# Joining each stage's linear term with its cube on DVE, and moving sums to POOL and ACT, in a two-phase recurrence and attention kernel

## The chip, the cores and the metric

The kernel runs on one core of a Trainium2 chip, in one launch. The metric is the device time in microseconds (us), as the median of several executions. A core has five engines that work side by side and wait for each other by semaphores: TensorE (PE; its weight loads are shown apart as PEld), VectorE (DVE), ScalarE (ACT), GpSimd (POOL) and SyncE (SP), which issues the DMAs. SBUF is the on-chip memory, PSUM the smaller memory that PE accumulates in.

## The reference

Two layers follow each other, each with a "condition" part and a feed-forward part, and both add to a residual. The first condition part is a time recurrence: 32 steps of a fourth-order Runge-Kutta scheme over a state q (128 x 256) with a companion p.

```python
def _derivative(q, p, drive, coupling, bias):
    i_couple = jnp.tanh(q) @ coupling.T
    dq = q - q ** 3 / 3.0 - p + drive + i_couple + bias
    dp = EPSILON * (q + ALPHA - BETA * p)
    return (dq, dp)

def _rk4_step(q, p, drive, coupling, bias):
    dq1, dp1 = _derivative(q, p, drive, coupling, bias)
    dq2, dp2 = _derivative(q + 0.5 * DT * dq1, p + 0.5 * DT * dp1, drive, coupling, bias)
    dq3, dp3 = _derivative(q + 0.5 * DT * dq2, p + 0.5 * DT * dp2, drive, coupling, bias)
    dq4, dp4 = _derivative(q + DT * dq3, p + DT * dp3, drive, coupling, bias)
    q_next = q + DT / 6.0 * (dq1 + 2 * dq2 + 2 * dq3 + dq4)
    p_next = p + DT / 6.0 * (dp1 + 2 * dp2 + 2 * dp3 + dp4)
    q_next = jnp.clip(q_next, -CLAMP, CLAMP)
    p_next = jnp.clip(p_next, -CLAMP, CLAMP)
    return (q_next, p_next)
...
x = x + _L0_ffn_ref(_L0_cond_ref(cond_2048, cond_2048, x, L0_cond_coupling, L0_cond_bias), L0_ffn_w_gate, L0_ffn_w_up, L0_ffn_w_down)
x = x + _L1_ffn_ref(_L1_cond_ref(x, cond_2048[:, None, :], L1_cond_W_emb, L1_cond_b_emb, L1_cond_g_norm, L1_cond_W_qkv, L1_cond_g_q, L1_cond_g_k, L1_cond_W_out), L1_ffn_w_gate, L1_ffn_w_up, L1_ffn_w_down)
```

The q of every step goes through a feed-forward network whose activations and weights are quantized in blocks of 32 (`_L0_ffn_ref`: gate, up, silu, down). The second layer is an attention over the 32 time steps with 16 heads of 16, in which queries and keys are normed and multiplied with weights `g_q` and `g_k`, and a feed-forward network with a Hadamard transform and 8-bit activations (`_L1_cond_ref`, `_L1_ffn_ref`).

## The kernel before

**Two phases.** Phase one runs the 32 time steps (`step`, L853) and, for each, the first feed-forward network (`ffn0`, L1238), the norm of the second layer and its value projection. Phase two (`tokens`, L1472) runs 32 groups of 128 tokens through attention and the second feed-forward network.

**A planner sets the order.** The functions do not issue instructions; they call `add(engine, cost, fn, reads, writes, ...)`, which records an item with its engine, an expected cost in us and the tiles that it reads and writes. `Work.run` then builds one order for all engines: a list scheduler that takes, at each point, the item with the least wanted time among those that can start. The wanted times are kept in the source as two long strings, `TIMES`, one for each phase. Costs serve this order alone; they change nothing in an instruction. An item marked `port=True` is kept from running beside another marked item; all tile operations of POOL carry the mark, and of DVE those that read two SBUF tensors or a large one in place. Where the planned PE is idle over 0.45 us, `keep_warm` puts matmuls on zeros in front of the next item (L1707).

**A stage of a step.** Each of the four stages has a PSUM tile `ps[i]` (256 columns) that collects the stage's sums: a first sum written by DVE (`nest`, L828, a `scalar_tensor_tensor`: in0 * scalar + in1), the drive and bias through PE (`inputs`, L860), the coupling (8 matmul records at L897, on tanh from ACT at L890), and the stage's own linear term, the state itself times a constant, through an eye matmul (`plus`, L881, the matmul at L883). Square (ACT, L891) times the state (POOL, L904) is the cube. A `nest` then joins `ps[i]` and the cube to the next state (`q2`, `q3`, `m4`), and the step ends with two saturating adds (L948) that give the new p (`z`) and the new q (a `states` tile). `p` and the sums `x`, `w`, `z` lie in slots of `ps_sum`, in PSUM, so that every `nest` has a PSUM tensor among its inputs.

```python
nest(ps[0], q, 2 * K[0] / h, p, rank)
inputs(0, RAW)
nest(ps[1], p, h / 2 * P2[0] / K[1], q, rank)
inputs(1, HALF_STEP)
nest(x, p, P3[0] * h / K[2], q, rank)
cube = slope(0, q)
nest(w, p, -LAST[0] / LAST[1], q, rank)
nest(z, p, -END[0] / END[1], q, rank)
nest(q2, ps[0], R2 * h / 2, cube, rank)
plus(1, 0, q2)
cube = slope(1, q2)
```

**Around it.** In `ffn0` POOL multiplies with block scales (L1258, L1301, L1309) and with the norm's gain (L1350), DVE takes maxima, products and clips (L1007, L992, L999, L1252, L1232, L1285). During the first steps the weights of the first network are quantized too, with POOL operations on 1024 columns (L1045, L1057, L1066). In `tokens` the queries are multiplied with `g_prod`, the product of the two weights, on POOL (L1512) before DVE transposes them (L1520); the exponential (L1552) and the silu (L1624) on ACT lie in different function tables, and each change between them is an ACT_TABLE_LOAD.

Of the kernel before, what the change touches and what calls it, by code (L numbers as in the profile page):

```python
# [15 lines left out]
AF = mybir.ActivationFunctionType  # L16
# [5 lines left out]
P = 128  # L22
# [83 lines left out]
class Work:  # L106
# [27 lines left out]
            "BIBKCNC9BWBVCiCWBuCTCaBzBfD7DjGGByDyEJEgEgE_CpGBEKEXFqF_GYEsFHGLGMFjGCGbGoIXHjHKIBHpHUJJKOL6J_LVJFJX"
            "K_KcJXKgKuMYNRMV9WBgBdDSCbDpCEDUCmCjCECLDqDtDpCID3D9CXBoDoCsEJE0EIDODjDYDOCpEAE5DVDdEUEuDLDqE5DdD-FQ"
            "FPH3DPFkFMFRFqFhE0FmFeGFGxHqI8GdGmHPHhIRIGH0H6I6IVJ6IuJUK4M6LILrM8ORL-MDN4LxLaMyObNWRFOFA3C-DQFJDdFU"
            "DxFOEIEhDiFeFjFbFPEFEoF0EIEzFKEoFOFAFmEfFHFkE0DVF-FlEwF1GJG8EnGBGkEuFSGOGLFvGGHzIJH9HkHGHhG_IHJPIYIv"
            "J5INJbIYJ5KNK3JbK6K1MDLZJsKJOhPONUNGR7MtQJO8QuNkRANpRrOOSDODDFEMF2GPFpGBFnGiFuGkFUGQGeGgGCFvHAHfG4H8"
            "HOF_GVHmHYG9GcGxGDHJH7H2G5GTIPH2GTHDH5GFGVGYHrJcHzIjItIbIcIOK5KfK8JeJVKPKRJzKMJCLKM5MALOKoM9L5NeMYN5"
            "NbSLO4O9ReN0RzPMRkPvRKOES7O-QUQ6GUG_H-H1H0HZGpHLH0GaGpGlHKH4HLGpHvGwHhH-HXI2HoHcHPHiH7H_IBIEHhHsHNIN"  # L140
            "I8IJHzHNHTI5HhIRIcNsJZJzJDIJKEKULHLIJoKkLFLULpMAMMN2MIMSMPMoMvNZNgOINkONMVRYPxQ4RaRASmRgS4RBSiQYS7SW"
            "RePRHjI7HvIgIgIHHuHxIJJ2JNJqIuIkJFJdIzIuIoJzItJ2IjJ2JWJqHRIUJxIOIbInJ7KKJvJpJTIkIyJSJQKgLJNXLxMLMELd"
            "NJMGMiOTMUMyPXNmNbN2O1QpNaO2PaPDPyQ8Q1PpPdQhN_RvRtRzRnQ1RGRdRwRGQsSBS2TJSgSdIQJ8JPJbKvKbKLKiKIKKJ_J_"
            "JlKTKPJwKWKdKTJMKyJqJhKWKQL0L2K4KVKiKnKaKPLJMNL2LZLWLALILsLGLcLwMfMrNPNXNVNxO1N-O6OMRnQIPdOKOURhQvQL"
            "QpQWR4R4RBRoS3RoPnRESTSJSnRiSVTfSyTESWThTKUyU7S8L8KQK8LrLMMKM5LxNBLbL9MsL_MrMNLsPCNvLjLwLeLuMfM1MYMz"
            "N_OCLsMzOHOdLtMfMLNHMBPhQLMZNCMzMuQUODNcOkNzPQOYQUOeOWOoS6QGS6OYPeSGRIROSVR-RnRkRiR-T3RWRXSrTZUDTeRm"
            "TuUWU0VsTfUGUvV_WRVOLIO1MMM4NAMONpMuQOQXN8NLMvMrNANGRfR5MnNEMuNUNLNJNoNmQiR8MxO-RPR4MaO5OVOeMxRNRcNq"
            "PuOFP9S8OVP-QeQbPzROP-QTPlR8S3S0RAQHRfT0SJSUSnShRrT0SaRqTtTpRsUZVGVxWhUNW0WuW2XUWrWXWfW7WoWlLZRHRDP9"
            "NOOhNcOiRERrNTPkPmQ8PvO8PxQiNlPwOyOCPVPuPjNuRVRCOZQvRlRWO3NeQJQiOrQlRROmQiPvQTPkPBR9QGRHR7RsR5QrSRSC"
            "RlT4SnSZShRbTVUNTmTUTfVWULVGUXUQSIXFX3XAY7XFXvYRZHYSYPXgZ8X-ZaYOMcQxRiQaPvQjPgQqRjRLPGQVQvQTQvQ3R7RZ"  # L150
            "QuQyQNQKR4QYSPQvRRRxQDRORhRPRBRdRTRTRMR5RmRNRAS2RWRERLRsRyRySNRmRURuSiTGTFUxUuTHU0UMUwVVVWVnVgVzVyWD"
            "WvWgTaZWXdXnZ2XYYzWlZIZXZoYDbEYCc9Z-O7S9RPRkRRRCRnS7Q_RMQwQPRvRqSNRmRQRARKRVReS9R_RQSTSAQ-RGRiRNRURN"
            "SISBTMSmRqSQSESQSZTDTaSOT9V2UsU1USUsTrQhUGUNUMW4W8UUUvV8X6X6XhXlXVY7XfX9YdYOYFb3YMYkcyYSbtZjcCahcmYw"
            "cQZVdGYkQHRnRFTpRoU4T2TnSdSaSZU6URUDTaTXTEShTXToTgShTuUAU3TJSfSyTjUWTFTETLTtV8UvTOTWTYTWUdUvVCSfU0VX"
            "V-VgVtWmWCSFW0WhWPY0YOWOXGWlYyYxZpYZZbZYaPa8Yma6badgZhZudJaEcvafd0bacsafd6c3dsdGQrSzSaUqU4ViU1VZU9T_"
            "TwVnVmVOV6UCULULUbUQV8UIVoW7VyUVUUUZUiV0V8V0UTU-W6WuVJVGVyVjWaWQW_WhVdX4Y0XSXGYOX0VoXAXQX_YBZ4XOXjaC"
            "XhY4YjZgbCZVZZZvZhaPcCdtbEbLeTcjeRcRegcpdwc9f5djfke8RmUUUzWVVoWFWWWrWGWIWIWXWtXMXPWOWiWuWGWkXOWPXgXX"
            "XdVyWiX6VqXMXLXEWyWpXyXyWVX4XHWkYiXgY1YGXLXVXnYRXpXYa_YdY5YPZaY_YfY8YdaQZbaabRb9ambobeZOdJapayfec8cj"
            "f1dvf4d_f_eGf5e7fue2fygARyWZWwXZXKXTX9YAXMYFWuVjXbWoYHXHYdYAXCZSXFX7Y0XJXQX8YuZIXMZEa7ZeXiXEXpXXXhZ6"
            "ZGXkZbYIYRX6Y8YWYwZBYoZ3XpYKYdYubbbabiYbZTc3bPbncxdQand4bsc5cvbvdKg0d8dtf3dqeqhFf4f7fGeafLeCfuiJY3YC"  # L160
            "YsX_XmYVYCY5ZMZGY9ZPYMYTYcXeb0b0Y8YTYJXuYPYvYvY4bebnYCZkbOaVY5YPYqa8YBbbbvY9ZKZia4Y-YyaqataobEbNaGZ9"
            "a4amd8cJcKb2bUctdFdneEeYe_e-f9eTdUf7eugffKetg2gogyghfzhFh1gFgSgWgqk1Y6ZWaPZ-YgZxYRaJbyc3Y3XRaYakbEYt"
            "c3cXYVXRb3Zja9bLb3Z2cyd0YaYzdcdWZSZKbdbeZ3djdMZEYsblcDc7aJczcwbwcKc3c_cObwctetd6dqczdHgKe8f3fYfpfAf9"
            "fwfgg9ggg3gAh1g9gzk8gshfhBiWgzhzhGisibl7YucBcCbUaKceaCbpcVcbaEa3cbbScGajd3dLZmbFbOaqbvcAb_akdBdWaUdM"
            "csdcbKb1bvcVbOdkdDb6d2ckbte3bxcsd7dBeTdmdee9dbd_fXgggOeceqfDfkebfYf0hDgMgrgKgtgwjjhBhwidi9jRhnjEiXiX"
            "iHiwiIjij6jHZkdAdOc1bKcdbxcJeBfdbrcBcYcad2buewe6c6dMcAc7cQcZddd3e1ead8d1egeeczdceGfod7eVf5dldGfLfJfH"
            "drezf7fAemgJgIg2gOgfgQgOg_gMgOgogjgShzhHhzgXj1ichVibl2j3jGjcjDm2jAjujgiNjYkak4kGktmqareEfAdwdleadOei"
            "fafkdqe9ere4dQdZewetdSejetdWdWeOefdoeJe-eTf6eUfJeGe8eZf2e1fTgpf9fleKfeggflgQgBfFgUg4gOi1h7hlhPh8hBh_"
            "hXh8hviNimhfjAiGkCjZikjHlikJk6khl0mOkwiQlIkkkZkolim4luo5dNfDf8fCeMf7f1fLfsfDf7fgfgfgfdfXeufFfIfzf-fS"
# [12 lines left out]
        (
# [361 lines left out]
def kernel(  # L544
# [283 lines left out]
    def nest(dst, in0, scalar, in1, rank, op1=ADD):  # L828
# [4 lines left out]
    b_p = Buf(ps_sum)  # L833
    add(
        DVE, 0.335,
        lambda: nc.vector.tensor_scalar(b_p.ap, condT, -ALPHA / BETA, -1.0, ADD, MULT),
        [b_condT], [b_p], rank=FIRST,
    )

# [930 lines left out]
```

## Time and profile before

| | |
|---|---|
| runs of the kernel | 794.51 us median of 3 (794.3 to 797.28) |
| the profiled execution | 793.31 us, its span 791.5 us |
| granted TensorE clock | 0.997 |
| PE busy | 742.4 us, 94% of the span |
| DVE busy | 693.8 us, 88% |
| POOL busy | 593.7 us, 75% |
| ACT busy | 533.9 us, 67% |
| eye matmuls L883 | 256 records, 78.7 us busy |
| cubes on POOL L904 | 128 (96 on `slim`, 31 on `states`, one on `condT`); the 96 take 771 ns each |
| ACT_TABLE_LOAD | 16 at L1552 and 16 at L1624, 1283 ns each |

The span is the time from the first to the last instruction of one execution; the rest of the execution's time lies around it. Busy time of an engine counts an instant once, however many records cover it; records of one engine overlap in its pipeline, so start-to-start distances are the better price where instructions stand close. An f32 matmul appears as two records. A group row gives the source line, the engine, the operation, what it writes and reads, the count, busy us and mean ns of one, and the idle time before it with what ended it.

### The profile page before, as it was taken

Reading aid. Unit: us, or ns where it says so; the run is one execution under the profiler, and the core shown is the slowest. Engines: PE = TensorE matmul, PEld = TensorE weight load, DVE = VectorE, ACT = ScalarE, POOL = GpSimd, SP = SyncE. Lnnn points to the kernel's source line nnn. Section 1 sums busy time; section 2 is a strip of 40 time slices with the busy share of each in tenths; the row PEclk is TensorE's granted clock in tenths of the full one; section 3 lists DMA queues with packets and bytes.
Section 4 is the critical chain, followed back from the end, with each engine's and each line's share of the span. In section 5 each row is a group of like instructions: output and inputs, shape, how many; then the busy total and the mean of one; then the engine's idle time right before and its main releaser. Section 6 shows DMA issues by size and latency. Waiting matters only on the chain.

```text
span 791.5 us, 26294 instructions
## 1 busy us (share of the span) xinstructions
PE 742.4 (94%) x10493; PEld 575.0 (73%) x10493; DVE 693.8 (88%) x1730; ACT 533.9 (67%) x1087; POOL 593.7 (75%) x963
## 2 busy tenths in 40 slices
PE   6879999999999999999887999999999999999996
PEld 5656688888888887788655566676777677777775
DVE  7888999999998998899837989899988999898894
ACT  4334467776766778998542577777877857688864
POOL 7968999878987788688727778877788788786700
PEclk9999999999999999999999999999999999999999
DMA  8222344323333253465330111433232532322552
GB/s 254 101 41 41 68 88 101 84 69 82 82 86 80 69 153 103 126 133 115 75 104 17 25 34 27 77 64 70 58 73 60 97 61 80 66 63 63 86 114 67
DMA packets 138522, 64.44 MB, mean 81 GB/s; under 512 B 103456, under 2 KB 137376, under 8 KB 138400
## 3 DMA queue, kind: packets, MB, share of 16 engines
q1 hardware_dynamic: 138400, 62.77, 34.6%
q8 instruction: 82, 1.34, 0.7%
q14 instruction: 40, 0.33, 0.1%
HBM read 25.77 MB, written 12.85 MB: 49 GB/s over the span
## 4 chain that ended last, share of the span: by engine, by line
PE 23%; DVE 16%; ACT 5%; POOL 3%; issue 3%; DMA 1%; ACTq 0%; DVEq 0%; POOLq 0%
PE ps_one L1483 4%; DVE wide L1647 4%; PE ps_two L1658 4%; PE ps_two L1616 3%; DVE tiny L1432 3%; PE ps_one L1560 3%; PE ps_one L1530 2%; PE ps_two L794 2%; DVE wide L1631 2%; PE ps_one L1583 2%; POOL wide L1647 1%; PE ps_one L1681 1%; ACT wide L1666 1%; DVE tiny L1545 1%; DVE tiny L1496 1%
## 5 line engine op out<-in xcount | busy, mean ns | idle before, releaser
L1647 POOL TENSOR_TENSOR wide<-wide 128x512 f32<-128x512 f32 x116 | 148.8, 1303 | 34.3 <-DVE wide L1647 16.8
L897 PE MATMUL ps_stage<-slim,coup 128*128 128x128 f32 x1024 | 139.1, 279 | 2.6 <-ACT slim L890 2.0
L897 PEld LDWEIGHTS ps_stage<-slim,coup 128*128 128x128 f32 x1024 | 127.8, 191 | 16.6 <-ACT slim L890 11.8
L904 POOL TENSOR_TENSOR slim<-slim,slim 128x256 f32<-128x256 f32 x96 | 74.0, 771 | 28.6 <-ACT slim L891 25.5
L883 PE MATMUL ps_stage<-slim,eye 128*128 128x256 f32 x256 | 78.7, 394 | 4.4 <-DVE slim L831 4.2
L1309 POOL TENSOR_TENSOR wide_bf<-mid,tiny 128x512 bf16<-128x512 fp8e4 x62 | 65.7, 1064 | 4.0 <-DVE mid L1232 3.7
L1301 POOL TENSOR_TENSOR mid<-mid,tiny 128x512 f32<-128x512 f32 x62 | 64.6, 1050 | 3.3 <-DVE tiny L999 1.7
L1658 PE MATMUL ps_two<-had_ffn,wide 128*128 128x128 f32 x512 | 63.7, 278 | 1.6 <-ACT wide L1653 0.8
L1658 PEld LDWEIGHTS ps_two<-had_ffn,wide 128*128 128x128 f32 x512 | 60.1, 192 | 5.8 <-ACT wide L1653 2.5
L1483 PE MATMUL ps_one<-w_qkv_sb,xnT 128*128 128x512 f32 x128 | 62.4, 616 | 0.7 <-ACT v_pad L1380 0.7
L890 ACT ACTIVATE slim<-slim 128x256 f32<-128x256 f32 x96 | 39.4, 410 | 29.0 <-DVE slim L831 28.7
L891 ACT ACTIVATE slim<-slim 128x256 f32<-128x256 f32 x96 | 39.1, 407 | 25.4 <-DVE slim L831 25.3
L883 PEld LDWEIGHTS ps_stage<-slim,eye 128*128 128x128 f32 x256 | 40.9, 190 | 20.9 <-DVE slim L831 17.2
L1647 DVE TENSOR_TENSOR wide<-wide 128x512 f32<-128x512 f32 x76 | 55.2, 762 | 0.0
L1666 ACT ACTIVATE wide<-ps_two,magic,tiny 128x1024 f32<-128x1024 f32 x32 | 38.6, 1205 | 24.2 <-DVE tiny L1440 14.6
L1232 DVE SCALAR_TENSOR_TENSOR mid<-mid,ps_sum 128x512 fp8e4<-128x512 f32 x64 | 43.3, 678 | 4.0 <-POOL mid L1301 3.8
L1432 DVE TENSOR_REDUCE tiny<-ps_two 128x1 f32<-128x1024 f32 x32 | 38.9, 1216 | 8.6 <-PE ps_two L1658 7.8
L1285 DVE TENSOR_TENSOR mid<-ps_gu,mid 128x512 f32<-128x512 f32 x64 | 43.5, 683 | 2.2 <-ACT mid L1281 1.8
L1653 ACT COPY wide<-ps_two 128x1024 f32<-128x1024 f32 x32 | 32.3, 1010 | 18.3 <-PE ps_two L794 17.7
L831 DVE SCALAR_TENSOR_TENSOR slim<-ps_stage,slim 128x256 f32<-128x256 f32 x96 | 40.1, 417 | 4.8 <-PE ps_stage L897 3.2
L1616 PEld LDWEIGHTS <-slim_bf 128*128 128x128 bf16 x256 | 23.9, 98 | 27.6 <-issue 7.4
L1281 ACT ACTIVATE mid<-ps_gu 128x512 f32<-128x512 f32 x64 | 37.7, 592 | 8.6 <-PE ps_gu L1273 8.3
(285 smaller groups left out, 2153.2 us busy)
## 6 DMA issues: line engine op xcount, KB each, us to landing
v_dram<-v_pad SPq DMA_DIRECT2D x32, 136.0 KB, 1.9
v_pad<-v_dram SPq DMA_DIRECT2D x32, 136.0 KB, 2.5
x_step<-in_x_dram SPq DMA_DIRECT2D x32, 128.0 KB, 2.1
x_add<-in_x_dram SPq DMA_DIRECT2D x32, 128.0 KB, 2.5
x_dram<-slim SPq DMA_DIRECT2D x32, 128.0 KB, 1.8
out_dram<-slim SPq DMA_DIRECT2D x21, 128.0 KB, 1.7
raws<-in_L_ffn_w_gate_dram SPq DMA_DIRECT2D x4, 512.0 KB, 5.7
raws<-in_L_ffn_w_up_dram SPq DMA_DIRECT2D x4, 512.0 KB, 6.5
```

Source lines behind the costliest of these rows:

```text
L883: PE, cost, lambda: nc.tensor.matmul(ps[i].ap, lhsT=eyes[eye], rhs=src.ap, start=False, stop=True, skip_group_check=True),
L897: nc.tensor.matmul(ps[i].ap[:, sl], lhsT=coup[COUP[i]][:, c, sl], rhs=two(th.ap)[:, c, :], start=False, stop=True, skip_group_check=True,)
L904: POOL, 0.685, lambda: nc.gpsimd.tensor_tensor(sq.ap, sq.ap, qi.ap, MULT),
L1285: DVE, 0.6, lambda act=act, it=it, pu=pgu[1]: tt(it.ap, pu.ap, act.ap, MULT),
L1301: lambda it=it, ks=ks, eng=eng: eng.tensor_tensor(blocks(it.ap), blocks(it.ap), spread(binv.ap[:, ks], BLOCK), MULT),
L1309: lambda b8=b8, ks=ks, sl=sl, eng=eng: eng.tensor_tensor(blocks(bq.ap[:, sl]), blocks(b8.ap), spread(bscl.ap[:, ks], BLOCK), MULT),
L1432: lambda: nc.vector.tensor_reduce(am.ap[:, 0:1], src.ap[:, :n], AX.X, ALU.max, apply_absolute_value=True),
L1483: nc.tensor.matmul(pqk.ap, lhsT=xnT_flat[:, c, tok], rhs=w_qkv_sb[:, c, : 2 * N], start=(c == 0), stop=(c == NC - 1),)
L1616: nc.tensor.matmul(pgu.ap[:, n * HALF : (n + 1) * HALF], lhsT=two(aT.ap)[:, c, :], rhs=w[:, sr, c, :], start=(c == 0), stop=(c == NC - 1),)
L1647: eng.tensor_tensor(dv[:, :, e, :], sv[:, :, 0, :], sv[:, :, 1, :], op)
L1658: nc.tensor.matmul(pfh.ap[:, sl], lhsT=iT.ap[:, sl], rhs=had_ffn, start=True, stop=True)
L1666: lambda: nc.scalar.activation(br.ap, pfh.ap, AF.Identity, bias=magic, scale=bs.ap[:, 0:1]),
```

## The change

In each stage the linear term no longer goes through PE: it is joined with the cube, so that the DVE operation computes (square + own) * state with a constant `own` for each stage. That takes the cube from POOL to DVE, and three of the four eye matmuls away; `plus(3, 2, q3)` remains. The first sum of a step becomes a scaled copy of p on ACT. The sum `x` is made by a scaling on ACT and an add on POOL, the first `z` (now `z1`) by a subtraction on POOL. For that p is carried times a constant `LAM`, and `p`, `x`, `z1` and the new p lie in SBUF (`slim`). In phase two the product with `g_prod` is no longer made by POOL on the queries but by ACT on the transposed queries, with a column of weights per partition (`g_col`, made once by three small DVE operations). Some recorded costs differ (0.27 to 0.307 for the drives, for instance), and both strings of wanted times are new, so that the order differs on every engine: 20 table loads are in the new order (32 before) and 249 matmuls on zeros (212 before). The new DVE operation and the `nest` calls are added without `port=True`.

```diff
+    LAM = END[0] / END[1]
+    R2, R3, R4 = -P3[2], -END[3] * LAM, -END[4] * LAM
...
-    b_p = Buf(ps_sum)
+    b_p = Buf(slim)
...
-        x, w, z = Buf(ps_sum), Buf(ps_sum), p
+        x, w, z, z1, pn = Buf(slim), Buf(ps_sum), Buf(ps_sum), Buf(slim), Buf(slim)
...
+        def pool_nest(dst, in0, scalar, in1):
+
+            part = Buf(slim)
+            add(ACT, 0.307, lambda: nc.scalar.mul(part.ap, in0.ap, scalar), [in0], [part], rank=rank)
+            add(
+                POOL, 0.685, lambda: nc.gpsimd.tensor_tensor(dst.ap, part.ap, in1.ap, ADD),
+                [part, in1], [dst], rank=rank, port=True,
+            )
...
-            add(
-                POOL, 0.685, lambda: nc.gpsimd.tensor_tensor(sq.ap, sq.ap, qi.ap, MULT),
-                [qi], [sq], rank=rank, port=True,
-            )
+            own = (R2 * K[0], -R3 * K[1] * EYES[0], -R4 * h * EYES[1], EYES[3])[i]
+            add(DVE, 0.335, lambda: stt(sq.ap, sq.ap, own, qi.ap, ADD, MULT), [qi], [sq], rank=rank)
...
-        nest(ps[0], q, 2 * K[0] / h, p, rank)
+        add(ACT, 0.36, lambda: nc.scalar.activation(ps[0].ap, p.ap, AF.Copy, scale=1.0 / LAM), [p], fills=[ps[0]], rank=rank)
...
-        nest(ps[1], p, h / 2 * P2[0] / K[1], q, rank)
+        nest(ps[1], p, h / 2 * P2[0] / K[1] / LAM, q, rank)
...
-        nest(x, p, P3[0] * h / K[2], q, rank)
+        pool_nest(x, p, P3[0] * h / K[2] / LAM, q)
...
-        nest(w, p, -LAST[0] / LAST[1], q, rank)
-        nest(z, p, -END[0] / END[1], q, rank)
+        nest(w, p, -LAST[0] / LAST[1] / LAM, q, rank)
+        add(
+            POOL, 0.685, lambda: nc.gpsimd.tensor_tensor(z1.ap, q.ap, p.ap, SUB), [q, p], [z1], rank=rank, port=True
+        )
...
-        plus(1, 0, q2)
...
-        nest(z, z, END[1] * R2 / END[2], q2, rank)
+        nest(z, z1, END[1] * R2 / END[2], q2, rank)
...
-        plus(2, 1, q3)
...
-        plus(3, 3, m4)
...
-        add_sat(z, z, m4, edge - CLAMP, edge + CLAMP)
+        add_sat(pn, z, m4, (edge - CLAMP) * LAM, (edge + CLAMP) * LAM)
...
+        own = Buf(tiny)
+
+        def column():
+            mask = own.ap[:, :D_HEAD]
+            nc.vector.tensor_reduce(mask, ident.rearrange("p (r d) -> p d r", d=D_HEAD), AX.X, ADD)
+            nc.vector.tensor_tensor(mask, mask, g_prod, MULT)
+            nc.vector.tensor_reduce(g_col, mask, AX.X, ADD)
+
+        add(DVE, 0.6, column, [b_gp], [own], fills=[b_gc], rank=rank)
...
-        add(
-            POOL, 0.69,
-            lambda: nc.gpsimd.tensor_tensor(
-                heads(qn.ap), heads(qn.ap), g_prod.unsqueeze(1).to_broadcast([P, HEADS, D_HEAD]), MULT
-            ),
-            [b_gp], [qn], rank=rank, port=True,
-        )
...
+        add(ACT, 0.32, lambda: nc.scalar.activation(qT.ap, qT.ap, AF.Copy, scale=g_col), [b_gc], [qT], rank=rank)
```

## The prediction

> **What bounds the kernel now.** I first cut the span by stage. The end of each time step is one instruction, the saturating add at L948 that writes a `states` tile. There are 32, the first starting at 21.7 us and the last at 381.8; the eighth ends at 114 us, so 114 to 382 holds 24 steps of 11.17 us. The view of busy time by window (sum of busy us of each engine, in the order PE, PEld, DVE, ACT, POOL):
>
> ```profile
> 0.00:114.00 114.00, 94.39 (x644) 72.76 (x645) 101.92 (x258) 51.83 (x140) 96.14 (x115) 1.00 0.41 98
> 114.00:382.00 268.00, 266.04 (x1898) 223.06 (x1897) 244.03 (x661) 203.29 (x557) 220.93 (x299) 1.00 0.41 98
> 382.00:405.00 23.00, 17.55 (x116) 12.42 (x114) 15.16 (x33) 12.16 (x34) 12.22 (x19) 1.00 0.36 89
> 405.00:760.00 355.00, 341.01 (x7658) 247.96 (x7656) 313.00 (x738) 249.59 (x339) 264.44 (x532) 1.00 0.29 62
> ```
>
> In the 24 steps PE is idle 2 us of 268 and DVE only 24. PE is the bound, DVE is second and close. In phase two (405 to 760) PE leads again, DVE has 88%. Who ends the step, from the timeline of one step (start, length, and in brackets the idle time before it and its releaser):
>
> ```profile
> 245.74 0.42 DVE L948 CUSTOM_DVE_ANT_0 states<-ps_stage,slim 128x256 f32<-128x256 f32 x1 [1.34 <-PE ps_stage L897]
> 246.20 0.43 DVE L831 SCALAR_TENSOR_TENSOR ps_stage<-states,ps_sum 128x256 f32<-128x256 f32 x1
> 246.54 0.42 DVE L831 SCALAR_TENSOR_TENSOR ps_stage<-ps_sum,states 128x256 f32<-128x256 f32 x1
> ...
> 250.38 0.68 DVE L1285 TENSOR_TENSOR mid<-ps_gu,mid 128x512 f32<-128x512 f32 x1
> 250.97 0.15 DVE L999 SCALAR_TENSOR_TENSOR tiny<-tiny,ps_sum 128x8 int32<-128x8 int32 x1
> ```
>
> DVE's idle time is a wait for the coupling matmuls. Records overlap in the pipeline, so I price by start-to-start: 0.33 us for a 256-wide DVE operation (246.20 to 246.54), 0.60 for a 512-wide one (250.38 to 250.97), about 0.1 for a tiny one.
>
> **PE: removed.** Three of the four eye matmuls of a step go (L883; 128 before, 32 after). Price from the same step:
>
> ```profile
> 249.44 0.59 PE L883 MATMUL ps_stage<-slim,eye 128*128 128x256 f32 x2
> 249.87 0.38 PE L865 MATMUL ps_stage<-ident,x_step 128*128 128x128 f32 x2
> ```
>
> 0.43 us from one start to the next, so 3 x 0.43 = 1.29 us a step: PE's floor falls from about 11.1 to 9.8 us. If nothing else became late, 32 x 1.29 = 41 us would be on offer.
>
> **DVE: one more operation, and another kind.** By the groups of the window DVE has 409 256-wide, 146 512-wide and 97 tiny operations in 24 steps: 17 x 0.33 + 6.1 x 0.60 + 4 x 0.1 = 9.7 us a step. After: four cubes come (L904 on POOL becomes a DVE operation), three leave (first sum to ACT, `x` and the first `z` to POOL): 10.0 us. That is no bound yet. But before, each DVE operation of a step reads at least one tensor in PSUM. After, `p`, `x`, `z1` and the squares lie in SBUF, and the order of the changed program shows 8 per step, 256 in all, that read two SBUF tensors: the four cubes, the sums for `ps[1]`, `ps[2]`, `w` and `z`.
>
> Here a rule of the Trainium skill speaks against the change. SBUF — State Buffer, section "SBUF: two separate sides": a DVE operation with two SBUF inputs and a GpSimd operation that reads SBUF share a port pair under an exclusive lock; the one that comes second stands still until the other is done. The trace has few such DVE operations, and there it agrees (three pairs from the timelines of DVE and POOL):
>
> ```profile
> 85.78 1.21 DVE L1061 CUSTOM_DVE_ANT_0 wide<-wide,wide 128x1024 f32<-128x1024 f32 x1
> 86.28 1.30 POOL L904 TENSOR_TENSOR slim<-slim,slim 128x256 f32<-128x256 f32 x1 [0.57 <-ACT slim L891]
> ...
> 94.63 0.41 DVE L1160 SCALAR_TENSOR_TENSOR gain<-gain,slim 128x256 f32<-128x256 f32 x1
> 94.88 0.76 POOL L904 TENSOR_TENSOR slim<-slim,slim 128x256 f32<-128x256 f32 x1 [0.46 <-ACT slim L891]
> ...
> 590.70 2.37 DVE L1647 TENSOR_TENSOR wide<-wide 128x512 f32<-128x512 f32 x2
> 590.95 1.56 POOL L1647 TENSOR_TENSOR wide<-wide 128x512 f32<-128x512 f32 x1 [1.81 <-DVE wide L1647]
> ```
>
> POOL's L904 takes 0.73 us alone; started during DVE's L1061 it took 1.30 and ended 0.59 after DVE's end (87.58 against 86.99). At L1160, the very form of the new operations, it ended 0.60 after DVE's end. So POOL needs the port for its last 0.59 us. In the last pair DVE lost: two L1647 took 2.37 us instead of 0.60 + 0.68. The 384 L831 with a PSUM input never took over 0.433 us, though POOL is 82% busy. A 512-wide POOL operation (1.05 us, L1301 and L1309) by the same 0.14 us lead holds the port 0.91 us.
>
> The price of one wait: after the change a step has on POOL three 256-wide operations holding 0.59 (`x`, `z1`, L1350), four 512-wide holding 0.91, and L1258 (0.62) holding 0.48. A DVE operation at a random moment waits on average the sum of hold squared over two, by the period: (3 x 0.174 + 4 x 0.414 + 0.115) / 11.2 = 0.20 us. Eight: 1.6 us a step. Bounds: 0 if each wait falls into time in which DVE would idle anyway; about 2.5 us if, where two or three such operations stand in a row (49 places in the new order), POOL takes the port in between each time. I take 1.6, since the planner isn't told that the new operations need the port (they are added without `port=True`), so its order doesn't keep them clear of POOL's. By the rows of L831 alone DVE would need 10.0 us a step, by the rule 11.6.
>
> **POOL and ACT.** POOL loses four cubes of 0.73 us and gains two sums: -1.5 us a step of 9.2 busy; it isn't the bound, so worth nothing itself, except that its gaps grow. ACT gains the first sum (0.38, as L1357) and the scaling for `x` (0.41, as L848): 8.5 busy us become 9.3 of 11.2, hidden behind DVE; uncovered it would be the next limit, since tanh and square stand in its queue. No DMA is added; SP keeps its 392 entries.
>
> **Latency of a stage.** Square on ACT, then 0.73 on POOL becomes square, then 0.42 on DVE. But the next sum also waits for tanh and 8 matmuls (1.1 us at L897), about as late as the cube was. So the shorter cube buys little, and a blocked cube holds all DVE work queued behind it.
>
> **Sum, 24 steady steps.** DVE 11.6 us plus 0.2 of the 1.5 us it had free (most of that was waiting for PE, which eases): 11.8 against 11.17, +0.6 x 24 = +14 us. **First 8 steps:** POOL runs 18 weight operations of 1.9 to 2.4 us (L1045, L1057, L1066), and a DVE operation meeting one waits longer: holds of 1.8, 2.2, 1.8 six times over 85 us give 0.4 us for each of 48, 19 us, against 8 x 1.5 = 12 us less POOL work where POOL was 84% busy: +6 us, rounded. **Phase two:** POOL loses the 0.73 us weighting of queries per group, ACT gains 0.41 x 32 = 13 us, and the new order has 20 table loads for 32: -12 x 1.28 = -15 us. PE work there is unchanged, so the most is PE's idle 14 us; I take -5, bounds -14 and +6 (an order worse than it looks). Column of weights: three tiny operations, nothing. Total +15: 793.3 (span 791.5 and 1.8 around it) becomes 808; the median of the runs, 794.5, lies 1.2 above the profiled one, within the rounding.
>
> **Rivals.**
> - **A, faster (0.23).** Waits mostly fall where DVE idles, 0.5 us a step count: 10.5 + 0.1 = 10.6, -0.57 x 24 = -14; first steps -3; phase two -5: 771. For it: PE is the strictest limit now and gets 1.3 us; POOL has more gaps. Against: DVE has just 24 us idle in 268.
> - **B, a draw (0.12).** 1.0 us of waits: 11.1 a step, -2; start +2, phase two -4: 790.
> - **Forecast (0.47).** 808, own range 800 to 820.
> - **C, much slower (0.18).** POOL and DVE alternate at the port, 2.5 us a step: 12.5 + 0.1, +1.4 x 24 = +34; start +12; phase two -3: 836.
> - That the change doesn't do what it says: matmuls, cubes and table loads are all in the built order, so only the order's quality is open; it lies in the ranges.
>
> Half a per cent (4 us) is what I count as no change. Faster: A and a quarter of B, 0.26; same: half of B and an edge of the forecast, 0.07; slower: 0.67. Range 771 to 834: it leaves out half of A and half of C.
>
> **What would show it.** DVE operations at the cube's line and at the nest line with two SBUF inputs: mean near 0.6 us instead of 0.42, longest over 1.2. POOL's 256-wide sums over 0.8. PE busy share of the steps below 95%, and L948 waiting for DVE's own queue, no longer for L897. ACT_TABLE_LOAD x10 and x10. The step at 11.8 us. I am wrong if the new operations keep 0.42 us while POOL works (then A), or if PE stays full.

## The result, and the profile after

The changed kernel takes **838.24 us** (median of 4 runs, 835.76 to 840.4); the kernel before, beside it on the same chip, 794.4 us (790.99 to 797.28). The ratio is 1.0553, with a 95% interval of 1.0501 to 1.0604: 44 us slower. The forecast was 808, its range 771 to 834. The profiled execution took 837.81 us, its span 835.9 us.

The span is cut by the same instruction as before, the saturating add that writes a `states` tile (now L955): the eighth ends at 125.4 us, the last at 427.6.

| | before | after | difference, us | forecast, us |
|---|---|---|---|---|
| end of step 8 | 114.2 us | 125.4 us | +11.2 | +6 |
| one step of steps 9 to 32 | 11.17 us | 12.59 us | 24 x 1.426 = +34.2 | +14 |
| after step 32 | 409.3 us | 408.3 us | -1.0 | -5 |
| sum | | | +44.4 | +15 |

So the time came in phase one. The changed kernel's view of busy time by window (columns as in the prediction: PE, PEld, DVE, ACT, POOL; then the granted clock, the DMA share and GB/s):

```profile
0.00:125.00 125.00, 88.99 (x561) 68.81 (x562) 115.54 (x243) 53.15 (x147) 78.10 (x87) 0.92 0.31 83
125.00:427.00 302.00, 260.73 (x1832) 205.75 (x1831) 298.80 (x705) 219.17 (x616) 213.61 (x261) 1.00 0.37 88
427.00:450.00 23.00, 16.75 (x105) 12.24 (x105) 16.61 (x39) 15.13 (x35) 13.49 (x20) 1.00 0.49 113
450.00:800.00 350.00, 336.54 (x7631) 245.74 (x7631) 309.62 (x732) 242.27 (x356) 243.30 (x500) 1.00 0.30 62
```

In the 24 steps DVE is now idle 3 us of 302, where it had 24 us of 268; PE fell from 99% to 86%, POOL's busy time a step from 9.2 to 8.9 us. DVE sets the step. What fills it is in the groups of that window, DVE alone (line, operation, out<-in, count | busy us, mean ns | idle before):

```profile
L914 DVE SCALAR_TENSOR_TENSOR slim<-slim,slim 128x256 f32<-128x256 f32 x72 | 41.3, 574 | 0.3 <-ACT slim L901 0.3
...
L832 DVE SCALAR_TENSOR_TENSOR slim<-ps_stage,slim 128x256 f32<-128x256 f32 x72 | 29.5, 409 | 0.0
L832 DVE SCALAR_TENSOR_TENSOR ps_sum<-slim,states 128x256 f32<-128x256 f32 x24 | 19.3, 803 | 0.1
L914 DVE SCALAR_TENSOR_TENSOR slim<-slim,states 128x256 f32<-128x256 f32 x24 | 18.9, 789 | 0.0
L832 DVE SCALAR_TENSOR_TENSOR ps_stage<-slim,states 128x256 f32<-128x256 f32 x24 | 18.0, 750 | 0.0
L832 DVE SCALAR_TENSOR_TENSOR ps_stage<-slim,slim 128x256 f32<-128x256 f32 x24 | 15.6, 649 | 0.0
L832 DVE SCALAR_TENSOR_TENSOR ps_sum<-slim,slim 128x256 f32<-128x256 f32 x24 | 13.7, 569 | 0.2
...
L955 DVE CUSTOM_DVE_ANT_0 states<-ps_stage,slim 128x256 f32<-128x256 f32 x24 | 9.8, 410 | 0.1
```

Two rows of the kernel before, in its 24 steps:

```profile
L831 DVE SCALAR_TENSOR_TENSOR ps_sum<-ps_sum,states 128x256 f32<-128x256 f32 x72 | 29.3, 425 | 0.2
...
L948 DVE CUSTOM_DVE_ANT_0 states<-ps_stage,slim 128x256 f32<-128x256 f32 x25 | 10.6, 423 | 12.3 <-PE ps_stage L897 8.5 <-POOL slim L904 1.5 <-POOL tiny L1340 1.4
```

In the changed kernel the row with `ps_stage` among its inputs is the same operation on the same number of elements, with one operand in PSUM: 409 ns. The rows with two SBUF inputs (`slim,slim`, `slim,states`) take 569 to 803. What they take over 415 ns each sums to 47 us, 1.96 us a step. L955 waits for nothing outside its engine any more (L948 before: 12.3 us of idle time). Two cases from the timeline of DVE and POOL (start, length):

```profile
242.90 1.27 DVE L914 SCALAR_TENSOR_TENSOR slim<-slim,slim 128x256 f32<-128x256 f32 x1
244.09 0.41 DVE L1268 TENSOR_TENSOR slim<-ps_turn,tiny 128x256 f32<-128x256 f32 x1
...
246.13 1.10 DVE L832 SCALAR_TENSOR_TENSOR ps_sum<-slim,slim 128x256 f32<-128x256 f32 x1
...
242.85 1.04 POOL L1317 TENSOR_TENSOR mid<-mid,tiny 128x512 f32<-128x512 f32 x1
243.85 0.90 POOL L1366 TENSOR_TENSOR slim<-slim,gain 128x256 f32<-128x256 f32 x1
...
245.89 1.05 POOL L1325 TENSOR_TENSOR wide_bf<-mid,tiny 128x512 bf16<-128x512 fp8e4 x1
246.90 0.80 POOL L1274 TENSOR_TENSOR slim_bf<-slim,tiny 128x256 bf16<-128x256 fp8e4 x1
```

The cube that starts 0.05 us after POOL's L1317 ends at 244.17, 0.28 after that one's end at 243.89; the next POOL operation, started in the meantime, takes 0.90 us where it took 0.73 before. The second pair shows the same, with L1274 at 0.80 for 0.62. DVE stands still, and then POOL does.

The timelines of the 24 steps say it for all 192 operations with two SBUF inputs: 54 of them started while POOL ran nothing and took 0.413 us on average, none over 0.42; 76 started with 0.45 us or more of a POOL operation still to run and took 0.942. So two SBUF inputs alone cost nothing here; meeting POOL does.

### The profile page after: what moved, and what is told of

It is laid out like the page before. It is cut to its first block, busy times and chain, and to the rows that moved or that the text cites. A ratio compares the mean times of both kernels' runs of the same rounds, so it can differ in the third digit from the quotient of the medians.

```text
span 835.9 us, 25989 instructions
## 1 busy us (share of the span) xinstructions
PE 730.5 (87%) x10338; PEld 554.5 (66%) x10338; DVE 763.2 (91%) x1765; ACT 549.3 (66%) x1171; POOL 548.5 (66%) x867
## 4 chain that ended last, share of the span: by engine, by line
PE 31%; DVE 11%; ACT 4%; issue 2%; POOL 1%; DMA 1%; SPq 0%; DVEq 0%; ACTq 0%
PE ps_one L1499 6%; PE ps_two L1667 6%; PE ps_two L1625 5%; PE ps_one L1569 4%; PE ps_two L795 3%; PE ps_one L1592 3%; PE ps_one L1539 2%; DVE wide L1656 2%; PE ps_one L1690 2%; DVE tiny L1448 2%; DVE wide L1640 1%; DVE tiny L1554 1%; PE ps_one L795 1%; PE ps_turn L1391 1%; ACT wide_bf L1679 1%
## 5 line engine op out<-in xcount | busy, mean ns | idle before, releaser
L907 PE MATMUL ps_stage<-slim,coup 128*128 128x128 f32 x1024 | 149.4, 290 | 39.0 <-ACT slim L900 37.8
L1325 POOL TENSOR_TENSOR wide_bf<-mid,tiny 128x512 bf16<-128x512 fp8e4 x62 | 68.0, 1102 | 23.2 <-DVE mid L1248 20.0
L1317 POOL TENSOR_TENSOR mid<-mid,tiny 128x512 f32<-128x512 f32 x62 | 67.9, 1106 | 17.0 <-DVE tiny L1006 16.9
L914 DVE SCALAR_TENSOR_TENSOR slim<-slim,slim 128x256 f32<-128x256 f32 x96 | 60.4, 629 | 0.3 <-ACT slim L901 0.3
L1289 PE MATMUL ps_gu<-w0uT,slim_bf 128*128 128x512 bf16 x128 | 38.6, 384 | 5.4 <-DVE mid L1301 4.3
L1289 PE MATMUL ps_gu<-w0gT,slim_bf 128*128 128x512 bf16 x128 | 38.4, 389 | 5.2 <-DVE mid L1301 2.8
L1014 DVE TENSOR_REDUCE tiny<-mid 128x16 f32<-128x512 f32 x64 | 42.9, 672 | 0.0
L1625 PE MATMUL ps_two<-w1gT,slim_bf 128*128 128x512 bf16 x128 | 38.2, 380 | 4.1 <-DVE wide L1640 2.6
```

Of the source, the lines that this page charges most:

```text
L907: nc.tensor.matmul(ps[i].ap[:, sl], lhsT=coup[COUP[i]][:, c, sl], rhs=two(th.ap)[:, c, :], start=False, stop=True, skip_group_check=True,)
L914: add(DVE, 0.335, lambda: stt(sq.ap, sq.ap, own, qi.ap, ADD, MULT), [qi], [sq], rank=rank)
L1014: lambda: nc.vector.tensor_reduce(dst_of(dst.ap), blocks(src_of(src.ap)), AX.X, ALU.max, apply_absolute_value=True),
L1289: nc.tensor.matmul(pg.ap, lhsT=two(aT.ap)[:, c, :], rhs=w[:, sl, c, :], start=(c == 0), stop=(c == NC - 1))
L1317: lambda it=it, ks=ks, eng=eng: eng.tensor_tensor(blocks(it.ap), blocks(it.ap), spread(binv.ap[:, ks], BLOCK), MULT),
L1325: lambda b8=b8, ks=ks, sl=sl, eng=eng: eng.tensor_tensor(blocks(bq.ap[:, sl]), blocks(b8.ap), spread(bscl.ap[:, ks], BLOCK), MULT),
```

## The experiments

**The theory**: the eight DVE operations with two SBUF inputs wait for POOL at a shared port, and this is the loss. **Rivals**: the cube's place in the chain of a stage; the order made by the new wanted times; the loss of PE work as cover. All times are medians of 4 runs (12 for e6_no_eye_matmuls), beside the kernel before on the same chip; the ratio has its 95% interval. Where an edit left costs and declared tiles alone, the order of the instructions on each engine stayed the same (all but e3 and e7).

| run | us | ratio to before | end of step 8 | step 9 to 32 | after step 32 |
|---|---|---|---|---|---|
| e1_squares_psum | 878.16 | 1.1039 (1.0989 to 1.1088) | 131.5 | 13.86 | 412.2 |
| e2_p_in_sbuf | 859.1 | 1.0806 (1.0765 to 1.0846) | 136.1 | 13.03 | 409.9 |
| e3_port_marks | 908.12 | 1.142 (1.1376 to 1.1464) | 147.8 | 13.04 | 444.3 |
| e6_no_eye_matmuls | 795.04 | 1.0011 (0.9993 to 1.0029) | 114.3 | 11.06 | 412.8 |
| e1b_cubes_one_sbuf | 808.55 | 1.0197 (1.0178 to 1.0216) | 116.2 | 11.85 | 406.7 |
| e1c_all_one_sbuf | 770.3 | 0.9713 (0.9699 to 0.9728) | 102.3 | 10.75 | 409.2 |
| e7_phase_two_alone | 821.31 | 1.0365 (1.0338 to 1.0391) | 116.1 | 11.15 | 435.7 |
| e10_eye_matmuls_back | 841.41 | 1.0613 (1.0598 to 1.0629) | 123.6 | 12.61 | 412.6 |
| f1_two_of_eight_left | 812.78 | 1.0235 (1.021 to 1.026) | 112.6 | 12.08 | 408.8 |
| f2_none_of_eight_left | 816.58 | 1.0283 (1.0258 to 1.0308) | 107.1 | 12.46 | 410.5 |
| f3_square_beside_constants | 801.79 | 1.0097 (1.0068 to 1.0126) | 110.8 | 11.63 | 411.2 |
| f4_square_beside_p | 824.58 | 1.0382 (1.0339 to 1.0425) | 114.5 | 12.36 | 410.0 |

**Squares in PSUM, first try.** The changed kernel, with the squares written into the unused half of the stage's PSUM bank, so that a cube has one SBUF input.

```diff
+    squares = [[Slot(slot.ap[:, N:], slot.bank) for slot in slots_] for slots_ in stages]
...
+            square = lambda: squares[i % 2][0].ap if True else sq.ap
...
-            add(ACT, 0.31, lambda: nc.scalar.activation(sq.ap, qi.ap, AF.Square, scale=CUBES[i]), [qi], [sq], rank=rank)
+            add(ACT, 0.31, lambda: nc.scalar.activation(square(), qi.ap, AF.Square, scale=CUBES[i]), [qi], [sq], rank=rank)
...
-            add(DVE, 0.335, lambda: stt(sq.ap, sq.ap, own, qi.ap, ADD, MULT), [qi], [sq], rank=rank)
+            add(DVE, 0.335, lambda: stt(sq.ap, square(), own, qi.ap, ADD, MULT), [qi], [sq], rank=rank)
```

> The changed kernel with each square written by ACT to PSUM instead of SBUF, so that the four cubes of a step read one SBUF tensor; every engine's order is the same. Theory (port waits on a DVE that has no idle time left): cubes fall from 629 to about 415 ns, a steady step from 12.6 to about 11.75 us, the whole to about 814 us. Rival (the new order, or the longer DVE list itself, is at fault): cubes may fall, the step stays near 12.6, about 838 us.

A miss: 40 us slower than the changed kernel. The cubes themselves fell to 423 ns, as the theory says, but new waits came with the tile. Its view of waits in the steps (engine, line and what it waited for: us, times, longest):

```profile
PEld ps_stage L909 <- ACT ps_stage L903: 62.0, 70, 1.6
...
PE ps_stage L909 <- ACT ps_stage L903: 37.7, 58, 1.5
DVE slim L916 <- PE ps_stage L909: 29.2, 39, 1.6
```

The coupling matmuls (L909) wait for the square (L903), and the cube (L916) for the matmuls. Matmuls use columns 0 to 255 of the tile, the square columns 256 to 511: no datum is shared, only the bank. The run tells nothing on what a step costs without such meetings.

**The kernel before with p in SBUF.** One part of the change alone: p's tile goes from PSUM to SBUF, in the kernel before, with its own order.

```diff
     b_p = Buf(ps_sum)
+    b_p.placed = Slot(tile_of("p_sbuf", [P, N]))
```

> The kernel before with one tile moved: p (and z, updated in place) lies in SBUF instead of PSUM. Same instructions, same order on every engine; eight DVE operations of a step now read two SBUF tensors. Theory: each waits about 0.24 us for POOL, 1.9 us a step, and DVE has 1.0 us idle: a steady step of 12.2 to 12.6 us for 11.17, the whole 825 to 840 us. Rival (the order of the changed kernel costs the time): no change, 794 us.

The strongest single showing: the tile's memory is all that differs, and the kernel before becomes 65 us slower. Groups of its steps:

```profile
L831 DVE SCALAR_TENSOR_TENSOR ps_sum<-p_sbuf,states 128x256 f32<-128x256 f32 x48 | 35.5, 756 | 0.2
...
L831 DVE SCALAR_TENSOR_TENSOR p_sbuf<-p_sbuf,slim 128x256 f32<-128x256 f32 x48 | 30.0, 625 | 0.1
L831 DVE SCALAR_TENSOR_TENSOR slim<-ps_stage,slim 128x256 f32<-128x256 f32 x72 | 29.8, 414 | 3.0 <-POOL slim L905 1.8 <-PE ps_stage L898 1.1
...
L831 DVE SCALAR_TENSOR_TENSOR ps_stage<-ps_sum,slim 128x256 f32<-128x256 f32 x24 | 10.0, 417 | 0.0
```

What touches `p_sbuf` beside another SBUF tile takes 574 to 773 ns (425 before); what has a PSUM operand stays at 414 to 417. Neither the new wanted times nor the joined cubes are in this kernel, so the wait needs neither. It costs more than I expected (825 to 840 us): 22 of the 65 us lie in the first eight steps, and each later step is 1.86 us longer, with waits of 2.1 us: little of the wait fell into time in which DVE had idled.

**Port marks.** The changed kernel with `port=True` on the eight, for the planner to keep them clear of POOL.

```diff
-            add(DVE, 0.335, lambda: stt(sq.ap, sq.ap, own, qi.ap, ADD, MULT), [qi], [sq], rank=rank)
+            add(DVE, 0.335, lambda: stt(sq.ap, sq.ap, own, qi.ap, ADD, MULT), [qi], [sq], rank=rank, port=True)
...
-        nest(w, p, -LAST[0] / LAST[1] / LAM, q, rank)
+        nest(w, p, -LAST[0] / LAST[1] / LAM, q, rank, port=True)
```

> The changed kernel with port=True on the eight DVE operations of a step, so that the planner keeps them clear of POOL's; the order differs, the wanted times are the same. Theory: the mean wait of the eight falls below 0.1 us, but the planner pays by placing others later: 815 to 835 us. Rival (the unmarked order costs nothing): 838 us or more.

70 us slower than without marks. The waits fell only from 1.96 to 1.4 us a step (cubes 549 ns), DVE's idle time rose from 0.13 to 0.8 us, and phase two, which holds no marked operation of these, takes 444 us instead of 408. The wanted times were made for another plan, and a different planned end of phase one gives phase two another order, too. So this run is no fair test of marks.

**PE's saving alone.** The kernel before without three of the four eye matmuls of a step, with nothing in their place, so that these terms are missing from the result.

```diff
-                PE, cost, lambda: nc.tensor.matmul(ps[i].ap, lhsT=eyes[eye], rhs=src.ap, start=False, stop=True, skip_group_check=True),
+                PE, cost, (lambda: nc.tensor.matmul(ps[i].ap, lhsT=eyes[eye], rhs=src.ap, start=False, stop=True, skip_group_check=True)) if (i, eye) == (3, 2) else lambda: None,
```

> The kernel before with three of the four eye matmuls of a step left out (the stages' own linear terms are missing from the result), all else in the same order. It prices what PE was worth. Theory (PE the bound, DVE 1.0 us behind it): PE falls to 9.8 us a step, DVE at 10.2 becomes the bound, a step of 10.3 to 10.7 us, the whole 772 to 782 us. Rival (PE was never the bound; the chain through tanh and coupling sets the step): 790 to 795 us. Full use of the saved PE time would give 755 us.

```profile
114.00:379.00 265.00, 247.06 (x1751) 196.49 (x1750) 243.88 (x660) 202.90 (x557) 219.93 (x298) 1.00 0.40 99
```

This is its window of the 24 steps. PE's busy time fell from 266 to 247 us and the weight loads from 223 to 196, and the step from 11.17 to 11.06 us. 19 us less PE gave 2.6 us in the steps, and none of it in the time (after step 32 it takes 412.8 us for 409.3; the cause of that stays open). PE was not the bound: the rival came. DVE still idles 21 of the 265 us (24 of 268 before).

**One SBUF operand each.** The changed kernel, whose order is kept; the second operand of the cubes (first run), of all eight (second run), is read from a column of constants in PSUM, so that these terms are missing from the result. Instructions and sizes stay.

```diff
-            add(DVE, 0.335, lambda: stt(sq.ap, sq.ap, own, qi.ap, ADD, MULT), [qi], [sq], rank=rank)
+            add(DVE, 0.335, lambda: stt(sq.ap, sq.ap, own, none.ap.to_broadcast([P, N]), ADD, MULT), [qi], [sq], rank=rank)
...
-        nest(ps[1], p, h / 2 * P2[0] / K[1] / LAM, q, rank)
+        nest(ps[1], p, h / 2 * P2[0] / K[1] / LAM, q, rank, no_in1=True)
```

> The changed kernel in which the four cube operations read a constant column in PSUM in place of the state (the cubes are zero in the result); same order on all engines, no new dependency. Theory (port): cubes at 415 ns, the waits of the other four stay near 1.1 us a step, a steady step of about 11.8 us, the whole about 815 us. Rival (the longer DVE list or the new order costs the time): 830 us or more.

> As the last, with the other four operations (sums for ps[1], ps[2], w and z) too reading that PSUM constant in place of their second tensor, so that no operation of a step reads two SBUF tensors (these terms too are missing from the result); same order. Theory: all waits gone, DVE at about 10.5 us of work a step: a steady step of 10.7 to 11.1 us, the first eight back near 115 us, the whole 783 to 795 us. Rival (something besides the port makes the changed kernel slow): 805 us or more.

Windows of the second run (first eight steps, the 24 others) and groups of its 24 steps:

```profile
0.00:102.00 102.00, 80.14 (x561) 61.82 (x562) 92.34 (x244) 52.79 (x147) 73.07 (x87) 1.00 0.37 101
102.00:360.00 258.00, 249.95 (x1828) 206.28 (x1828) 252.70 (x705) 216.53 (x614) 194.34 (x261) 1.00 0.43 102
...
L915 DVE SCALAR_TENSOR_TENSOR slim<-slim,ps_sum 128x256 f32<-128x256 f32 x96 | 40.2, 418 | 1.3 <-ACT slim L902 0.3
...
L833 DVE SCALAR_TENSOR_TENSOR ps_sum<-slim,ps_sum 128x256 f32<-128x256 f32 x48 | 20.5, 427 | 0.3
L833 DVE SCALAR_TENSOR_TENSOR ps_stage<-slim,ps_sum 128x256 f32<-128x256 f32 x48 | 20.5, 426 | 0.1
```

All eight are back at 418 to 427 ns, and the kernel takes 770.3 us, 68 less than the changed one: 24 x (12.59 - 10.75) = 44 in the steps, 23 in the first eight, nothing in phase two. The cubes alone are worth 30 of it. The order and the place of the cube are those of the changed kernel, so neither is the loss. A caution goes with the number: ps[1], ps[2], `w` and `z` lose a dependency with the operand, so 770 us may be less than the change would take without the port.

**Phase two alone.** Phase one of the kernel before, phase two of the changed one with its wanted times.

```diff
-            POOL, 0.69,
-            lambda: nc.gpsimd.tensor_tensor(
-                heads(qn.ap), heads(qn.ap), g_prod.unsqueeze(1).to_broadcast([P, HEADS, D_HEAD]), MULT
-            ),
...
+        add(ACT, 0.32, lambda: nc.scalar.activation(qT.ap, qT.ap, AF.Copy, scale=g_col), [b_gc], [qT], rank=rank)
```

> The kernel before with phase two of the changed one: weights of queries by ACT, its wanted times for phase two, 20 table loads. Phase one as before but for the three small operations of the column of weights. Theory: phase two is bound by PE's list, which is the same: 789 to 796 us. Rival (fewer table loads and a lighter POOL pay): under 787 us.

Inconclusive: its phase two takes 436 us with the same 20 table loads, where the changed kernel's takes 408. The plan of phase two begins where that of phase one ends, and from another beginning these wanted times give another order (the traces of the two show different orders on DVE and ACT). What the new phase two is worth is read from the two kernels themselves: 1 us.

**The eye matmuls back.** The changed kernel with the linear terms of stages 1 to 3 on PE again, inside the coupling's item, `own` = 0, cubes still on DVE.

```diff
+                if i:
+                    nc.tensor.matmul(ps[i].ap, lhsT=eyes[(None, 0, 1, 3)[i]], rhs=qi.ap, start=False, stop=True, skip_group_check=True)
...
-            own = (R2 * K[0], -R3 * K[1] * EYES[0], -R4 * h * EYES[1], EYES[3])[i]
+            own = (R2 * K[0], 0.0, 0.0, 0.0)[i]
```

> The changed kernel with the linear terms of stages two to four back on PE: three eye matmuls a step in front of the coupling, the constant in the joined DVE operation zero; all else, and the order, the same. Theory (DVE is the bound, PE has 1.7 us idle a step): 834 to 845 us, no change. Rival (the saved PE time is worth its 1.3 us a step and hides part of the loss): 860 us or more.

The steps take 12.61 us for 12.59, and the ratio's interval (1.0598 to 1.0629) meets that of the changed kernel (1.0501 to 1.0604). The matmuls that the change saves cost nothing in its order either.

**Versions that keep the arithmetic and leave the port.** f1 is the changed kernel with each square in a PSUM slot that PE never touches (half a bank, beside w), p and z in one PSUM slot, and a copy of p by ACT for POOL's `z1`; ps[2] and z still read two SBUF tiles. f2 sends these two through PSUM as well, with two more ACT copies (last two lines).

```diff
+    P_SLOT, W_SLOT, SQ = ps_sum[2], ps_sum[0], ps_sum[1]
...
+            nc.scalar.copy(p_copy, p.ap)
+            nc.gpsimd.tensor_tensor(z1.ap, q.ap, p_copy, SUB)
...
+                nc.scalar.copy(dst.ap, src.ap)
+                stt(dst.ap, dst.ap, scalar, q2.ap, MULT, ADD)
```

> The changed kernel with its whole arithmetic and PE order, in which six of the eight DVE operations of a step get one operand from PSUM, without a wait added on purpose: ACT writes each square into one PSUM quarter-bank that PE never touches; p and z share one PSUM slot as in the kernel before, so the two operations that read p are off the port; POOL's z1 takes p from a copy that ACT makes (one ACT operation of about 0.31 us more a step). Left on the port: ps[2] from x and q2, and z from z1 and q2. Port theory, from the run with all eight off it (770.3 us, 10.75 us a step) and 0.24 us of wait for each that stays: 10.75 + 2 x 0.24 = 11.2 us a step, end of step 8 near 106 us, time 770 + 2 x 0.24 x 24 + 23 x 2/8 = 788 us, range 780 to 798; both of the eight still at 600 to 750 ns, the cubes at 420. Rival, that the run of 770 us owed its time to the operand that it left out (a dependency less, not a port less): the cubes and the operations on p gain nothing here and the time stays above 820. Third, ACT in the way (the square and w share a PSUM bank, so that one waits for the other): the step stays above 11.8 us with the DVE operations themselves at 0.42, and ACT named as the releaser.

> As the run before, and the last two taken off the port too: just ahead of the two DVE operations ACT copies x into ps[2] and z1 into z (PSUM), and DVE works there in place. Three ACT operations of about 0.3 us more a step than in the changed kernel. Port theory with ACT's copies hidden: all eight at 0.42, 10.75 us a step, 770 us, range 766 to 785, below the kernel before. Rival, that ACT's copies are on the path ([...]ps[2] is written only after DVE has read stage 0 from the same bank, so that the copy, the square behind it and the cube of stage 1 come later by 0.3 us and a semaphore): 0.3 to 0.6 us a step dearer, 780 to 795, no better than with two left on the port.

Both beat the changed kernel (by 25 and 22 us), neither the one before. The operations behave as the theory says (f1: ps[2] at 690 ns and z at 622, the other six at 413 to 428), but it is the third case that came: DVE's idle time is back, 0.82 us a step in f1 and 1.57 in f2. In f2 it is also worse than the rival's 780 to 795 us; between 125 us and the end of the steps, 12.1 and 7.8 us of its idle time are waits for the two added ACT copies. In f1, from the groups of DVE after 125 us:

```profile
L832 DVE SCALAR_TENSOR_TENSOR ps_sum<-ps_sum,states 128x256 f32<-128x256 f32 x23 | 9.8, 428 | 4.9 <-ACT p_copy L930 2.9 <-ACT ps_sum L905 1.2 <-ACT slim L889 0.7
L832 DVE SCALAR_TENSOR_TENSOR ps_stage<-ps_sum,states 128x256 f32<-128x256 f32 x23 | 9.8, 425 | 3.2 <-ACT p_copy L930 3.1
```

These two sums read p, and wait for ACT, which reads p for the copy that POOL gets (L930): two readers of one tile. From the groups of ACT between 120 and 360 us:

```profile
L905 ACT ACTIVATE ps_sum<-slim 128x256 f32<-128x256 f32 x60 | 22.7, 378 | 3.4 <-DVE slim L832 3.3
...
L921 ACT ACTIVATE ps_stage<-ps_sum 128x256 f32<-128x256 f32 x20 | 7.7, 387 | 4.0 <-DVE mid L1256 2.7 <-DVE slim L1256 0.7 <-DVE ps_sum L963 0.3
```

The scaled copy of p (L921), the first sum of a step, waits for DVE's clip of the other network (L1256). The clip reads a constant in PSUM, in the same bank as p: again two reads that take turns. `ps_sum[2]` is the half bank beside these constants. So f3 (first added line: the square beside the constants) and f4 (second: the square beside p and z) change the placement alone, same instructions and order:

```diff
-    P_SLOT, W_SLOT, SQ = ps_sum[2], ps_sum[0], ps_sum[1]
+    P_SLOT, W_SLOT, SQ = ps_sum[0], ps_sum[1], ps_sum[2]
...
+    P_SLOT, W_SLOT, SQ = ps_sum[0], ps_sum[2], ps_sum[1]
```

> The kernel of 812.8 us (six of the eight off the port) with only its PSUM placement changed: p, z and w in one bank as in the kernel before, ACT's squares in the quarter-bank beside the constants that DVE's clips read. In the run of 812.8 us ACT's copies of p waited for those clips (named DVE mid L1256), some 0.3 us a step each, though both only read. If engines take turns on one PSUM bank whatever they do there: these waits go from the copies of p and come back at the squares (four a step against the clips): 11.8 to 12.4 us a step, 805 to 820 us. If it is only the copies of p at the head of a step that cost, 11.2 to 11.5 us a step, 785 to 797 us. If placement has no part in it and the rest of the gap is the operand that the run of 770 us left out (a dependency less), unchanged at 12.1 us and 813 us, with no wait named at the squares.

> The same with p, z and the squares in one bank that neither PE nor the clips touch, and w, which DVE alone uses, beside the constants. If engines take turns on a bank, this placement leaves the fewest meetings (a square against the z terms and the two operations that read p): ACT's waits for the clips go, 11.2 to 11.6 us a step, 785 to 800 us, clearly below the kernel with the squares beside the constants. If placement has no part, 12.1 us a step and 813 us like the other.

The same two rows of ACT's groups in f3, from 125 to 400 us,

```profile
L905 ACT ACTIVATE ps_sum<-slim 128x256 f32<-128x256 f32 x69 | 26.1, 379 | 6.3 <-DVE mid L1256 2.5 <-DVE slim L832 1.5 <-DVE slim L1256 1.4
...
L921 ACT ACTIVATE ps_stage<-ps_sum 128x256 f32<-128x256 f32 x22 | 8.6, 390 | 1.4 <-PE ps_stage L911 1.0 <-DVE ps_sum L963 0.2
```

and in f4:

```profile
L905 ACT ACTIVATE ps_sum<-slim 128x256 f32<-128x256 f32 x66 | 25.2, 382 | 9.3 <-DVE ps_sum L832 5.0 <-DVE ps_sum L963 1.9 <-DVE slim L832 1.7
...
L921 ACT ACTIVATE ps_stage<-ps_sum 128x256 f32<-128x256 f32 x23 | 8.9, 386 | 4.0 <-DVE slim L918 2.8 <-DVE tiny L1007 0.6 <-DVE ps_sum L963 0.4
```

In f3 the wait leaves the copy (L921) and a part of it comes back at the square (L905), now for the clips; in f4 the square waits for DVE's work on z, and the copy of p for the cube that reads the square. 23 us lie between two placements of the same instructions. My guess that f4 would have the fewest meetings was wrong. f3, at 801.8 us, is the best version that keeps the arithmetic: 36 us better than the changed kernel, 1% slower than the one before. Its step of 11.63 is 0.4 above what 10.75 and the two remaining waits (710 and 591 ns, +0.47 together) make. By its trace 0.3 of that is idle time of DVE (0.52 us a step, 0.22 in the 770 us run), and the largest named waits in it are for ACT's copy of p, 3.1 us in the 24 steps. How the rest splits between meetings in a bank and the dependencies that the 770 us run left out was not separated.

## Why the prediction was half right

**Right: the sign, and its reason.** Eight operations a step wait for POOL; the second of a pair stands still. The Trainium skill gives the shared port pair as the reason (SBUF — State Buffer, "SBUF: two separate sides"), the trace of before had three cases, and e2, e1b and e1c show it from both sides: the wait comes with the tile's memory and goes with it. The signs that I named were there: means of 569 to 803 ns and a longest of 1.28 us in the 24 steps, POOL's sums over 0.8 us (829 and 893 ns), PE below 95%, L955 no longer waiting for matmuls, 10 and 10 table loads.

**Wrong, the largest term: "10.0 us a step" for DVE without waits.** It is 252.7 / 24 = 10.53 in e1c, and 12.45 - 1.96 = 10.49 in the changed kernel itself. The price holds: most 256-wide operations in the timeline of e1c's steps start 0.33 us apart too. The list was wrong. I took over the operations of before, but the new order leaves feed-forward work of the first eight steps to the others. One of its groups of 512-wide operations, first before, then in e1c:

```profile
L1007 DVE TENSOR_REDUCE tiny<-mid 128x16 f32<-128x512 f32 x48 | 32.5, 677 | 0.2
...
L1015 DVE TENSOR_REDUCE tiny<-mid 128x16 f32<-128x512 f32 x52 | 35.4, 682 | 0.0
```

In all, the 24 steps of e1c hold 157 512-wide operations for 146, and 5 more 256-wide ones of that network: (11 x 0.60 + 5 x 0.33) / 24 = 0.34 us a step. The rest is in part operations that use the result of the one in front: they start 0.46 us after it, as the first two of the quoted timeline do (245.74 and 246.20). A check was at hand: the sum gave 9.7 us a step for the kernel before, and its first view has 244.03 us in 24 steps, 10.17. Worth 24 x 0.53 = 13 us.

**The wait of 0.20 us.** It is 0.245 by the durations (1.96 us over eight) and 0.23 by the difference of steps (1.84 over eight). The estimate from POOL's holding times was 13 to 18% low. 6 to 9 us. Part of it may be that POOL, itself stopped by DVE, is at the port longer (its 512-wide operations went from 1050 to 1108 ns).

**The first eight steps: +6, measured +11.** The waits were 23 us, not 19: DVE is busy 115.5 of the first 125 us, and 92.3 of 102 in e1c, with the same idle time (9.5 and 9.7). e1c ends step 8 at 102.3, 11.9 earlier than before, which is the relief of 12 us that I had priced; but that it fits is partly luck, since 11 of the 33 512-wide DVE operations of these steps, about 7 us, were put off to the later ones. The granted clock was 0.92 there, 1.00 before and in e1c. e10, with 0.97 and the same busy time of DVE, ends step 8 1.8 us earlier, so up to that much of the +11 may be the clock; it was not separated. In the 24 steps the clock was 1.00 in all these runs.

**Phase two: -5, measured -1.** The twelve table loads went, 15 us of ACT, and bought nothing.

These misses add up to 13 + 6 + 5 + 4 = 28 of the 29 us between +15 and +44. Case C's time of 836 came out nearly right, but by waits of 2.5 us a step that were not there: luck.

**Wrong in kind: "PE is the bound", and 41 us "on offer".** e6 and e10 give nothing for the same matmuls. The 99% was no bound: three matmuls a step fewer took 7% of PE's busy time away and 1% of the step. The Trainium skill has the rule (Perfetto Trace Analysis, "Identifying the Most-Contended Engine"): the busy share of matmuls is not a good measure of how much room TensorE has; the busy share of its weight loads is, beside the operations done. By that rule the first view read PE 223 of 268, 83%, and DVE 244, 91%: DVE first. The runs agree: one operation more on DVE and its waits set the step, 19 us less on PE did not. Rival A, whose 771 us happens to be what e1c takes, argued from PE's 1.3 us; the 23 us that e1c gains on the kernel before cannot be those, since e6 has them and gains nothing. They are idle time of DVE: in phase one it is busy as long in both (346 and 345 us) and idle 36 us before, 15 in e1c. How that splits between the relief of POOL and the lost dependencies stays open.

## What to carry to other kernels

Before a tensor is moved from PSUM to SBUF, count the DVE operations that then read two SBUF tensors, and the busy share of POOL beside them: here 0.24 us each, with POOL 70 to 80% busy. Count an engine's list in the new order, not in the old one, hold the sum for the old one against its busy time, and do not take PE's busy share for a bound. In a kernel whose order is tuned by a list of wanted times, a part can't be taken out of a change without the list that was made for it: two such trials lost 27 and 36 us in a phase two that has the changed kernel's instructions.

## What was not expected

Putting a tensor back into PSUM is not free of meetings either. In e1 matmuls and squares took turns over disjoint columns of one bank (62 and 38 us of waits on PE's two rows, 29 on DVE), and in f1, f3 and f4 even two readers did: in f1 DVE's sums waited for ACT's reading of the same p, and the same instructions took 801.8, 812.8 or 824.6 us by which slot lay beside which. The Trainium skill names this (PSUM — Partial Sum Buffer, "PSUM bank collisions raise a hardware error"): engines have to be kept apart by bank, reads against reads included. What the traces show is the price of it, as waits on semaphores in the built program; a collision itself no run here shows.
